# Convolution steps placed by a table of points, and the border terms at a later point, in a kernel of self-attention and local attention

## The chip, the cores and the metric

The kernel runs on one core of a Trainium2 chip. The metric is the device time of one execution in microseconds (us), the median of three; lower is better. In the trace the engines are PE (TensorE, matmuls), PEld (its weight loads), DVE (VectorE), ACT (ScalarE), POOL (GpSimd) and SP (SyncE, which issues transfers).

## What is computed

Two layers on an image batch of 4 x 64 x 64 points with 256 channels, all in float32. The reference, cut to what matters:

```python
# layer 0: attention of every point of an image to every other
q, k, v = x @ Wq + bq, x @ Wk + bk, x @ Wv + bv        # 256 -> 32, 32, 256
attn = softmax(einsum('bnd,bmd->bnm', q, k))           # 4096 x 4096 per image
x = gamma * (attn @ v) + x

# layer 1
perceived = depthwise_conv3x3(x, w_perc) + b_perc      # 3 outputs per channel: 768
hid = gelu(w_up1 . perceived + b_up1)                  # 768 -> 512
h = x + (w_up2 . hid + b_up2)                          # 512 -> 256
q, k, v = split(w_qkv . h + b_qkv)
scores = [(q * k shifted by (dy, dx)).sum(-1) / 16 for the 9 neighbours, zeros outside]
out = h + sum(softmax(scores)[i] * v shifted by i)
```

## The kernel before

**Slots and points.** The image rows are worked in blocks of 8 rows (512 points), 8 blocks to an image, so 32 slots in all. Slot `s` runs layer 0's attention for block `s`, and with it layer 1's stages for earlier blocks: the convolution for block `s - 2`, the pointwise layers, guides and scores for block `k = s - 3`, the local attention's output for block `a = s - 5`. [...]

A slot has 16 points. At each point the program issues, in this order: the energies of keys two points ahead (`energy`, every other point, line 294); the exponential of them on ACT (`weight`, L302); the jobs of layer 1 listed for this point; `product`, the attention product of this point (4 matmuls, each of which stands as two records, L313, tile `acc`); the sum of the weights on DVE (`add_up`, L327, tile `den`); and then a number of convolution steps on DVE. At the end of the slot the sums are turned and inverted and the finished block is written back to the image buffer `xp`.

**The convolution.** `perceive` hands out single DVE instructions. A tap is a multiply-add of a shifted window (L468), a tile of 6 outputs by 8 taps: 48 in a slot. The ninth tap of an output is its first, done on ACT with the bias (`begin`, L464), and is issued when the step after it is asked for. The outputs come in three groups of two, each group in one `perc` buffer; after the 16 taps of a group come 4 additions or subtractions (L474, "mixes"), which prepare the operands of a matrix product by Strassen's scheme with 7 products (Winograd's form). So a group is 20 steps, and a slot 60. There are four `perc` buffers: group 1 of a block takes the one that held group 0 of the block before, which the first pointwise layer (`hidden_part`, points 0 to 3) reads.

**The jobs by point.** For block `k` the two pointwise layers and the guides (the product of query and key weights, applied to `h`) are done in parts named for their products:

| point | jobs | |
|---|---|---|
| 0 to 3 | `hidden_part`: products a, bc, then de, gf, for d = 0 and d = 1 | DVE gathers them (L580), ACT applies GELU (L596) |
| 4, 5 | `local_product` for block a: the output's two halves, `lo` | DVE scales (L1026), POOL adds up for a check and adds `h` (L186, L1036) |
| 5 | `update_mix` | DVE (L660, L661) |
| 6 to 8 | `update_part`: dx_ab, dx_cd and dx_eg, dx_f | DVE gathers into `h` (L537); with ab also L678 and L679, which replace two blocks of `hid` by mixes of them |
| 8 | end of part f: bias and residual (L689), `guide_mix` (L798), `border_terms` (L855, L856) | DVE |
| 9, 10 | `guide_part`: g_ab, g_cd, then g_eg, g_f | DVE gathers into `lq` (L537, L539) |
| 11, 12 | `scores`, halves 0 and 1 (tile `s`, L924) | ACT exponential, POOL mask and sums |
| 13 | `local_values` (L883) | |
| 14 | `border`: a matmul over the tile `edge`, which `border_terms` writes | ACT, POOL |

`border_terms` works out the score of the points outside the image: two DVE instructions for each of two sides, and for each of two halves of a row more in the first and the last block of an image (4 instructions, or 8).

The second pointwise layer's product cd reads the blocks of `hid` that L678 writes in part ab; g_cd reads the tiles `gmix` of `guide_mix`; the scores read `lq`.

In the last block of each of the first three images the next image's projections (query, key and value, L226 and L260) are done in the same slot, every other point: slots 7, 15 and 23.

The lines that set the convolution's pace, before:

```python
n_mixed = NPC * (TAPS - 1) + MULT * len(MIXED)      # 60
to = min(n_steps, -(-(point + 1) * n_steps // (points - 2)))
if point < 3:
    to = min(to, n_mixed // MULT)
while stepped < to:
    next(conv, None)
    stepped += 1
```

## Time and profile before

The kernel takes 3490.17 us (3489.78 to 3491.19). The profiled execution has a span of 3487.6 us.

| what | value |
|---|---|
| PE busy | 3454.0 us, 99% of the span |
| PEld busy | 1995.1 us, 57% |
| DVE busy | 2796.8 us, 80% |
| ACT busy | 1063.4 us, 30% |
| POOL busy | 694.3 us, 20% |
| granted PE clock | 0.999 |
| L313 attention product | 4096 records, 1838.6 us |
| L468 convolution taps | 1554 instructions, 1166.7 us, mean 0.811 us |
| L474 convolution mixes | 360 instructions, 174.3 us, mean 0.498 us |
| L327 sum of the weights | 480 instructions, 604.6 us, mean 1.259 us |
| transfers | mean 19 GB/s |

Matmuls are pipelined and their ends are modelled, so the busy share of PE covers short waits; they are read from the distance between starts in the timeline. In the timeline a line gives the start in us, the length of the merged stretch, the engine, the line of the program, the operation, the output and inputs, the shape and the count, and in brackets the idle time before it with what ended it.

### The profile page before, as it was taken

To read this page: it belongs to the slowest core of one execution; us is meant where nothing else is said; L and a number is where in the kernel's file an instruction comes from. 1 tells how busy PE (TensorE), PEld (TensorE's weight loads), DVE (VectorE), ACT (ScalarE), POOL (GpSimd) and SP (SyncE) were. 2 spreads that over 40 slices of the span, in tenths; PEclk is the share of its full clock that TensorE was granted. 3 is DMA by queue.
4 is the path that set the end of the run, shared out by engine and by line. 5 is a ranking of instruction groups with operands and counts; after the bars stand their busy time and mean duration, and the time that the engine had idled before them with its cause. 6 is when DMAs were issued, how large, how long until landed. Compare 5 with 4: busy or idle time off the path is not lost. (4 is left out here: it accounts for less than half of the span.)

```text
span 3487.6 us, 34030 instructions
## 1 busy us (share of the span) xinstructions
PE 3454.0 (99%) x12726; PEld 1995.1 (57%) x12726; DVE 2796.8 (80%) x4249; ACT 1063.4 (30%) x1328; POOL 694.3 (20%) x829
## 2 busy tenths in 40 slices
PE   9999999999999999999999999999999999999998
PEld 5445555555555555566555555556655555555655
DVE  2388888768888988876888889887688888888886
ACT  3233333323332233332333322333233333223331
POOL 2010112111221221121112212212121121221133
PEclk9999999999999999999999999999999999999999
DMA  4000000120000000011000000001100000000000
GB/s 106 7 4 10 7 9 16 32 47 20 9 16 7 16 16 16 22 25 46 16 9 16 10 13 16 16 22 31 39 16 16 16 10 7 16 16 17 7 7 25
DMA packets 93276, 67.06 MB, mean 19 GB/s; under 512 B 65872, under 2 KB 71248, under 8 KB 92976
## 3 DMA queue, kind: packets, MB, share of 16 engines
q1 hardware_dynamic: 92432, 64.42, 6.8%
q8 instruction: 102, 1.67, 0.2%
q14 instruction: 70, 0.57, 0.1%
q10 hardware_dynamic: 672, 0.39, 0.0%
HBM read 43.62 MB, written 18.81 MB: 18 GB/s over the span
## 5 line engine op out<-in xcount | busy, mean ns | idle before, releaser
L313 PE MATMUL acc<-p,v 128*128 128x512 f32 x4096 | 1838.6, 594 | 0.2 <-DVE o L378 0.2
L313 PEld LDWEIGHTS acc<-p,v 128*128 128x128 f32 x4096 | 768.2, 190 | 795.8 <-issue 779.6
L468 DVE SCALAR_TENSOR_TENSOR perc<-xp,wperc,perc 128x512 f32<-128x512 f32 (+2 forms) x1554 | 1166.7, 811 | 7.0 <-ACT perc L464 7.0
L302 ACT ACTIVATE p<-e 128x1024 f32<-128x1024 f32 x512 | 523.9, 1023 | 1695.0 <-PE e L294 776.9
L327 DVE TENSOR_TENSOR den<-den,p 128x1024 f32<-128x1024 f32 x480 | 604.6, 1259 | 85.4 <-ACT p L302 83.6
L186 POOL TENSOR_TENSOR watched<-watched,lo 128x256 f32<-128x256 f32 x124 | 136.8, 1103 | 1015.8 <-DVE lo L1026 1010.7
L948 POOL TENSOR_TENSOR lp<-lp,near 128x396 f32<-128x396 f32 x60 | 77.5, 1291 | 1137.9 <-ACT lp L944 1132.9
L294 PE MATMUL e<-qa,ka 32*128 32x512 f32 x2048 | 291.9, 640 | 0.0
L474 DVE TENSOR_TENSOR perc<-perc 128x256 f32<-128x256 f32 x360 | 174.3, 498 | 7.2
L294 PEld LDWEIGHTS e<-qa,ka 32*128 32x128 f32 x2048 | 80.0, 182 | 166.2 <-issue 164.2
L573 PE MATMUL hid_de<-perc,wmix 128*128 128x256 f32 x720 | 165.2, 379 | 0.0
L573 PEld LDWEIGHTS hid_de<-perc,wmix 128*128 128x128 f32 x720 | 136.8, 190 | 43.7 <-issue 21.5
L580 DVE TENSOR_TENSOR hid<-hid_bc,hid 128x512 f32<-128x512 f32 x60 | 41.5, 692 | 147.4 <-PE hid_bc L573 147.3
L596 ACT ACTIVATE hid<-hid,bup 128x512 f32<-128x512 f32 x120 | 80.1, 715 | 214.3 <-DVE hid L580 214.3
L464 ACT ACTIVATE perc<-xp,bperc,wperc 128x512 f32<-128x512 f32 x192 | 145.4, 807 | 0.0
L969 POOL TENSOR_TENSOR lsum<-lsum,lp 128x99 f32<-128x99 f32 x168 | 132.0, 792 | 11.0
L1014 PEld LDWEIGHTS lo<-lp,lv 128*128 128x128 f32 x732 | 102.9, 191 | 35.1 <-issue 27.0
L883 PE MATMUL lv<-wlv,h 128*128 128x256 f32 x520 | 122.4, 379 | 0.0
L186 POOL TENSOR_TENSOR watched<-watched,o 128x256 f32<-128x256 f32 x128 | 109.6, 856 | 43.2 <-DVE o L378 35.7
L302 ACT ACT_TABLE_LOAD x60 | 77.0, 1283 | 134.1 <-PE e L294 134.1
L260 PE MATMUL v<-wv,xc 128*128 128x256 f32 x512 | 116.3, 380 | 0.1
L883 PEld LDWEIGHTS lv<-wlv,h 128*128 128x128 f32 x520 | 98.7, 190 | 27.5 <-issue 15.5
(191 smaller groups left out, 3398.8 us busy)
## 6 DMA issues: line engine op xcount, KB each, us to landing
xp<-in_x SPq DMA_DIRECT2D x30, 528.0 KB, 4.1
xc<-in_x SPq DMA_DIRECT2D x56, 256.0 KB, 3.7
out<-lo SPq DMA_DIRECT2D x56, 256.0 KB, 2.1
qa<-packed SPq DMA_DIRECT2D x124, 64.0 KB, 2.0
out<-res SPq DMA_DIRECT2D x8, 256.0 KB, 2.0
ka<-st SPq DMA_DIRECT2D x124, 16.0 KB, 1.8
packed<-st SPq DMA_DIRECT2D x31, 64.0 KB, 1.9
wup<-in_w_up SPq DMA_DIRECT2D x1, 1536.0 KB, 6.8
```

Of the source, the lines that this page charges most:

```text
L186: nc.gpsimd.tensor_tensor(at, at, values[:, i : min(n, i + C)], ALU.add)
L260: nc.tensor.matmul(ps[:, i * C : (i + 1) * C], lhsT=xc[:, kin, bass.ts(2 * pair + i, P)], rhs=wv[:, kin, :], start=(kin == 0), stop=(kin = ...
L294: nc.tensor.matmul(e[:, j, :], lhsT=key[rows, :], rhs=queries[s][rows, :], start=True, stop=True,)
L302: nc.scalar.activation(p, energies[s, G][:, 2 * half : 2 * half + 2, :], AF.Exp)
L313: nc.tensor.matmul(accs[s][c], lhsT=v[:, 2 * half + i, bass.ts(c, P)], rhs=p[:, i, :], start=(first and i == 0), stop=(G == NG - 1 and hal ...
L327: nc.vector.tensor_tensor(den, den, p, ALU.add)
L464: nc.scalar.activation(acc, win, AF.Identity, bias=bperc[:, half, j : j + 1], scale=wt)
L468: nc.vector.scalar_tensor_tensor(acc, win, wt, acc, ALU.mult, ALU.add)
L474: nc.vector.tensor_tensor(t[:, to, :], t[:, a, :], t[:, b, :], op)
L573: nc.tensor.matmul(ps[:, n * C : (n + 1) * C], lhsT=w(j), rhs=mixes[s, j][:, kind, :], start=(j == 0), stop=(j == MULT - 1),)
L883: nc.tensor.matmul(ps[:, half * C : (half + 1) * C], lhsT=keys_of(s, t, half, kin), rhs=wlv[:, kin, :], start=(kin == 0), stop=(kin == CH ...
L969: nc.gpsimd.tensor_tensor(to, to, near_ws[block, half][:, t_, of, :], ALU.add)
```

## The change

Two edits of order; no operation is added or dropped.

The pace of the convolution follows a table of steps per point instead of an even spread over 14 points, in all slots but the last. The table has few steps at points 6 to 9, where the second pointwise layer and the guides are done, and more at the points before. The spread before comes to 5, 4, 4, 5, 4, 4, 4, 5, 4, 4, 5, 4, 4 and 4 steps at points 0 to 13. It is meant to let DVE serve the products of points 6 to 10 sooner.

`border_terms` is no longer called at the end of `update_part`'s part f (point 8) but as a job of its own at point 13, ahead of `local_values`. The call in `update`, which serves the last blocks, stays.

```diff
@@ update_part
                 guide_mix(s)
-                border_terms(s)
@@ jobs
-                job(scores, k, 1) + job(local_sum, k - 1), job(local_values, k, 0), job(border, k), [],
+                job(scores, k, 1) + job(local_sum, k - 1),
+                job(border_terms, k) + job(local_values, k, 0), job(border, k), [],
@@ the slot's loop
             n_steps, stepped = n_mixed, 0
+            share = [7, 7, 6, 6, 6, 5, 2, 1, 1, 2, 3, 5, 5, 4, 0, 0]
...
-                to = min(n_steps, -(-(point + 1) * n_steps // (points - 2)))
+                if slot < NSLOT - 1:
+                    to = sum(share[: point + 1])
+                else:
+                    to = min(n_steps, -(-(point + 1) * n_steps // (points - 2)))
                 if point < 3:
                     to = min(to, n_mixed // MULT)
```

## The prediction

> **What bounds the kernel now.** I read the page's busy shares first, then the list of waits, then the timeline of one ordinary slot (slot 8, 786.7 to 889.8 us) engine by engine, and beside it a slot with a bordering block (slot 10).

> ```profile
> PE 3454.0 (99%) x12726; PEld 1995.1 (57%) x12726; DVE 2796.8 (80%) x4249; ACT 1063.4 (30%) x1328; POOL 694.3 (20%) x829
> ```

> TensorE is the bound: a slot takes what its matmuls take, plus the few places where they wait. Here is TensorE in slot 8 (start, length, operation), from point 3 to point 9:

> ```profile
> 819.51 3.60 PE L313 MATMUL acc<-p,v 128*128 128x512 f32 x8
> 835.37 1.99 PE L525 MATMUL dx_ab<-hid,wup 128*128 128x256 f32 x8
> 837.20 3.60 PE L313 MATMUL acc<-p,v 128*128 128x512 f32 x8
> 840.64 1.03 PE L525 MATMUL dx_cd<-hid,wmix 128*128 128x256 f32 x4
> 849.65 3.60 PE L313 MATMUL acc<-p,v 128*128 128x512 f32 x8
> 853.09 1.17 PE L525 MATMUL g_ab<-h,wg 128*128 128x256 f32 x4
> 854.84 1.10 PE L525 MATMUL g_cd<-gmix,gmix 128*128 128x256 f32 x4 [0.58 <-DVE gmix L798]
> ```

> The reader is to see two things. An acc group of eight is followed 3.44 us later by the next group: no wait before dx_cd. But g_ab to g_cd takes 1.75 us, where four such matmuls take 0.86 (dx_cd, 840.64 to 841.50): 0.89 us is waited for gmix. The same in slot 10 before the scores:

> ```profile
> 1069.79 1.88 PE L313 MATMUL acc<-p,v 128*128 128x512 f32 x4
> 1072.36 1.66 PE L924 MATMUL s<-lq,h 128*128 128x198 f32 x8 [0.70 <-DVE lq L539]
> ```

> Why gmix is late is on VectorE's timeline of slot 8:

> ```profile
> 819.71 0.69 DVE L580 TENSOR_TENSOR hid<-hid_gf,hid 128x512 f32<-128x512 f32 x1 [1.44 <-PE hid_gf L573]
> 820.32 1.22 DVE L327 TENSOR_TENSOR den<-den,p 128x1024 f32<-128x1024 f32 x1
> 821.45 2.07 DVE L468 SCALAR_TENSOR_TENSOR perc<-xp,wperc,perc 128x512 f32<-128x512 f32 x3
> 823.56 0.88 DVE L474 TENSOR_TENSOR perc<-perc 128x256 f32<-128x256 f32 x2
> 826.02 0.69 DVE L1026 TENSOR_TENSOR lo<-lo,lrden 128x512 f32<-128x512 f32 x1 [1.58 <-PE lo L1014]
> 829.50 2.42 DVE L468 SCALAR_TENSOR_TENSOR perc<-xp,wperc,perc 128x512 f32<-128x512 f32 x2
> 833.15 1.10 DVE L661 TENSOR_TENSOR hid<-hid 128x512 f32<-128x512 f32 x1
> 834.17 1.74 DVE L327 TENSOR_TENSOR den<-den,p 128x1024 f32<-128x1024 f32 x1
> 835.84 3.75 DVE L468 SCALAR_TENSOR_TENSOR perc<-xp,wperc,perc 128x512 f32<-128x512 f32 x4
> 839.51 0.68 DVE L678 TENSOR_TENSOR hid<-hmix,hid 128x512 f32<-128x512 f32 x1
> 848.19 3.40 DVE L468 SCALAR_TENSOR_TENSOR perc<-xp,wperc,perc 128x512 f32<-128x512 f32 x5
> 851.50 0.42 DVE L537 TENSOR_TENSOR h<-dx_f,h 128x256 f32<-128x256 f32 x1
> ```

> dx_f's matmuls end at 849.65, but its gather (L537) starts at 851.50, behind five convolution steps. These twelve lines carry the forecast as well: after its last idle 1.58 us before lo, VectorE works without a pause to L678, and L678 ends at 840.19. L678 writes the block that dx_cd's first matmul reads at 840.64. So dx_cd has about 0.45 us to spare, hardly more than the 0.15 us between gmix's end (854.69) and g_cd's start.

> [...] 99% busy holds the 0.89 us wait. [...] while GpSimd sums lo, one step starts at 829.50 and the next 1.68 us later, where steps elsewhere follow each other every 0.66 us.

> **The change, part by part.** Steps per point go from 5 4 4 5 4 4 | 4 5 4 4 | 5 4 4 4 to 7 7 6 6 6 5 | 2 1 1 2 | 3 5 5 4. The sum stays 60: 48 taps at 0.66 us and 12 mixes at 0.43. Nothing is removed, so only order can pay. The last slot keeps the old rule.

> *Few steps at points 6 to 9.* VectorE then reaches dx_f's gather before the matmuls end. From that gather to the third gmix it needs 3.19 us (851.50 to 854.69), say 3.4 from dx_f's end, while acc and g_ab give TensorE 3.44 + 0.86 = 4.30 us. The wait before g_cd goes. Counting every start-to-start distance above what the form needs when nothing waits, g costs 0.96 us and s 0.24 us of an ordinary slot more than in the three slots with projections, 7, 15 and 23. There are 23 full ordinary slots: 23 x 0.96 = 22.1.

> *Border's terms to point 13.* 4 instructions (8 in a bordering block) of some 0.2 us leave point 8, where they stand before the den sum and the guides' gathers. At point 13 VectorE has finished the guides, and border (matmul at point 14) is their only reader. With fewer steps at 9 and 10 the scores' wait goes too: 0.24 in 16 slots, 1.02 in six with a bordering block, 0.59 in slot 12, 0.88 in slot 3: 3.8 + 6.1 + 0.6 + 0.9 = 11.4. Gain so far 33.5 us.

> *More steps at points 0 to 2.* Hidden by VectorE's pauses: at point 0 two more taps are 1.3 us, the de gather comes at 802.2 instead of 800.8, and the hidden product that takes its bank starts at 806.9. At point 1 three more taps end at 809.8; the bc gather waits for TensorE until 811.17 anyway. At point 2, taps and four mixes end near 815.9, before de at 817.12. So point 3 starts as before. Cost nothing.

> *More steps at points 3 to 5.* Here there is no room. Before: 13 steps, 9 taps and 4 mixes. After: 17, of which 16 taps and one mix, since the four mixes of group 0 are done at point 2 and group 1 begins at point 3. Also, group 1's first taps are ScalarE's (L464), and at point 3 they now stand behind the two GELUs: these start at 820.44 and 821.07, so the first taps end near 822.5 and 823.2. They can't be earlier, as the perc buffer is free only after hid_gf. VectorE, ready at 821.45, waits 1.1 us. From 820.32:
> - point 3: den 1.13; wait 1.13; six taps 4.0 (the second waits a little): lo's scaling at 826.6, not 826.02.
> - point 4: scaling 0.61, den 1.13, six taps 3.97, and 1.94 lost to GpSimd (as in slot 8: L474 0.52 and 0.41, L468 1.01): the second scaling at 834.2, not 831.84.
> - point 5: scaling 0.60, hmix and L661 1.41, den 1.13, four taps 2.65, one mix 0.42, 1.94 lost to GpSimd: L678 at 842.3, not 839.51.
> L678 ends at 843.0, and with the 0.15 us of the g_cd release dx_cd starts at 843.15, not 840.64: a new wait of 2.5 us. Queued behind dx_cd on TensorE are eg, the next acc groups and everything else[...]. It isn't earned back: the slot behind it is matmuls back to back. In the projection slots TensorE has 3.6 to 5.5 us more at points 3 and 5, and VectorE idled 5.03 us before lo (slot 15), so no wait. Slots 3 and 4 have no lo and no GpSimd work there: I reckon 0.7 and 0.5. Bounds: were GpSimd's 3.9 us lost in pauses, no wait at all; with another 0.7 us for tap order and releases, 3.2 a slot. I take 2.5: 23 x 2.52 + 1.2 = 59.

> Sum: 3490.2 - 33.5 + 59 = 3516 us. An ordinary slot goes from 103.1 to 104.4 us.

> **Rivals.** (A) The early points keep up, the waits at g_cd and s vanish: 3490.2 - 33.5 = 3457. For it: VectorE is busy 89 of 103 us in a slot, so slack exists. Against: of that slack none lies between lo and L678 beyond 1.58 us. (B) The new wait is about 1.4 us, equal to the 33.5 us gained: 3490. It takes VectorE 1.1 us earlier at L678, for instance no wait for ScalarE's first taps; against it, their place behind the GELUs. (C) A larger loss: L678 later still, or a second wait (eg for hmix, exp for a p buffer) beside it: at 3.3 us a slot, 3490.2 - 33.5 + 77 = 3534. Against: dens run two or more points ahead of the buffers that exp takes.

> **Numbers.** Forecast 0.72, A 0.11, B 0.06, C 0.11. The forecast's own spread, 2.0 to 3.1 us per slot, is 3504 to 3529; with part of C up to 3534 and some room towards B, 3500 to 3534 holds 8 in 10. Slower takes the forecast and C: 0.83; within 0.2% is B with its edges: 0.06; faster 0.11.

> **What would show it.** Right: the timeline has dx_cd waiting some 2.5 us for L678 in the 23 ordinary slots, none before g_cd and at most a trace before s, the first L464 of group 1 directly after the GELUs with a VectorE pause near 1.1 us at point 3, slots of 104.4 us, and 137.0 with projections. Wrong: L678 before 840 in slot 8's time (then A), or a wait elsewhere, such as exp for p or a bank at points 0 to 2.

## The result and the profile after

The changed kernel takes 3546.11 us (3545.12 to 3548.19), the kernel before 3490.68 us in the same comparison: a ratio of 1.016, 95% interval 1.0142 to 1.0177. It is slower, as forecast, but by 55.4 us, where 26 us were forecast, and above the stated range of 3500 to 3534 us.

```profile
PE 3475.9 (98%) x12726; PEld 2022.4 (57%) x12726; DVE 2811.6 (79%) x4249; ACT 1063.4 (30%) x1328; POOL 653.9 (18%) x829
```

The shares on the page hardly move: TensorE goes from 99% to 98%, while the span grows by 57.2 us. The same stretch of slot 8 shows why. The slot now starts at 791.44 us. First VectorE from point 3 on, in the timeline:

```profile
825.09 1.22 DVE L327 TENSOR_TENSOR den<-den,p 128x1024 f32<-128x1024 f32 x1
827.28 4.11 DVE L468 SCALAR_TENSOR_TENSOR perc<-xp,wperc,perc 128x512 f32<-128x512 f32 x6 [0.98 <-ACT perc L464]
831.30 0.68 DVE L1025 TENSOR_TENSOR lo<-lo,lrden 128x512 f32<-128x512 f32 x1
833.04 6.01 DVE L468 SCALAR_TENSOR_TENSOR perc<-xp,wperc,perc 128x512 f32<-128x512 f32 x6
838.97 0.68 DVE L1025 TENSOR_TENSOR lo<-lo,lrden 128x512 f32<-128x512 f32 x1
842.97 3.73 DVE L468 SCALAR_TENSOR_TENSOR perc<-xp,wperc,perc 128x512 f32<-128x512 f32 x4
847.08 0.68 DVE L678 TENSOR_TENSOR hid<-hmix,hid 128x512 f32<-128x512 f32 x1
```

L678 starts 55.64 us after the start of the slot; in the kernel before it was 52.83 (839.51 - 786.68). It is 2.81 us later, behind the taps of points 3 to 5: in this stretch VectorE's instructions start in the order in which the program issues them (den 825.09, taps 827.28, lo 831.30 and so on to L678 847.08). Then TensorE in the same slot:

```profile
841.97 3.60 PE L313 MATMUL acc<-p,v 128*128 128x512 f32 x8
847.82 1.80 PE L525 MATMUL dx_cd<-hid,wmix 128*128 128x256 f32 x4 [2.26 <-DVE hid L678]
849.41 1.91 PE L525 MATMUL dx_cd<-hid,wup 128*128 128x256 f32 x4
851.12 1.25 PE L525 MATMUL dx_eg<-hmix,wmix 128*128 128x256 f32 x4
```

Two things are to be seen. dx_cd starts 5.85 us after the acc group began, instead of 3.44: it waits 2.42 us. (The bracket says 2.26, as it counts from the modelled end of the last matmul.) And the matmuls behind the wait are slow: the second group of four dx_cd takes 1.71 us to the next start (849.41 to 851.12), where the same four took 0.86 before. Slot 10, with the same wait, doesn't have this:

```profile
1060.04 1.13 PE L525 MATMUL dx_cd<-hid,wmix 128*128 128x256 f32 x4 [2.26 <-DVE hid L678]
1061.01 1.03 PE L525 MATMUL dx_cd<-hid,wup 128*128 128x256 f32 x4
```

The list of stretches of 3.41 us, cut so that the changes of the clock fall on the cuts, names it. Its columns are the stretch, its length, TensorE's busy time and instructions, the granted share of TensorE's clock, and two columns on transfers:

```profile
841.32:844.73 3.41, 3.41 (x11) 1.00 0.00 0
844.73:848.14 3.41, 1.15 (x3) 1.00 0.55 154
848.14:851.56 3.42, 3.42 (x10) 0.50 0.00 0
851.56:854.97 3.41, 3.41 (x13) 1.00 0.00 0
```

The stretch that holds the whole wait has TensorE busy for 1.15 us of 3.41. In the next 3.41 us the clock is halved, which costs 1.69 us (eight matmuls at 0.43 instead of 0.22 us). Comparing the starts of all 23 full ordinary slots: every one waits 2.42 to 2.44 us before dx_cd, 18 are halved once and take 106.1 us, and 5 (slots 5, 10, 16, 21 and 26) take 104.4. The waits before g_cd and before the scores are gone from the list of waits; it has instead

```profile
PE dx_cd L525 <- DVE hid L678: 52.9, 25, 2.3
```

### The profile page after: what moved, and what is told of

It is laid out like the page before. It is cut to its first block, busy times and chain, and to the rows that moved or that the text cites. A ratio compares the mean times of both kernels' runs of the same rounds, so it can differ in the third digit from the quotient of the medians.

```text
span 3544.8 us, 34087 instructions
## 1 busy us (share of the span) xinstructions
PE 3475.9 (98%) x12726; PEld 2022.4 (57%) x12726; DVE 2811.6 (79%) x4249; ACT 1063.4 (30%) x1328; POOL 653.9 (18%) x829
## 4 chain that ended last, share of the span: by engine, by line
PE 82%; DVE 15%; ACT 2%; issue 1%; POOL 0%; DMA 0%; SPq 0%; ACTq 0%; POOLq 0%; DVEq 0%
PE acc L313 40%; DVE perc L468 9%; PE e L294 6%; PE hid_gf L573 4%; PE hid_de L573 4%; PE hid_bc L573 4%; PE lv L882 3%; PE v L260 3%; PE hid_a L573 3%; PE s L923 2%; PE dx_cd L525 2%; DVE den L327 2%; PE dx_eg L525 2%; PE hid L605 1%; ACT hid L596 1%
## 5 line engine op out<-in xcount | busy, mean ns | idle before, releaser
L313 PE MATMUL acc<-p,v 128*128 128x512 f32 x4096 | 1838.6, 594 | 0.3 <-DVE o L378 0.3
L313 PEld LDWEIGHTS acc<-p,v 128*128 128x128 f32 x4096 | 768.2, 190 | 795.8 <-issue 779.8
L468 DVE SCALAR_TENSOR_TENSOR perc<-xp,wperc,perc 128x512 f32<-128x512 f32 (+2 forms) x1554 | 1174.6, 818 | 32.4 <-ACT perc L464 32.4
L327 DVE TENSOR_TENSOR den<-den,p 128x1024 f32<-128x1024 f32 x480 | 600.9, 1252 | 85.0 <-ACT p L302 83.2
L186 POOL TENSOR_TENSOR watched<-watched,lo 128x256 f32<-128x256 f32 x124 | 143.9, 1161 | 1063.2 <-DVE lo L1025 1058.1
L573 PE MATMUL hid_de<-perc,wmix 128*128 128x256 f32 x720 | 165.2, 379 | 0.0
L573 PEld LDWEIGHTS hid_de<-perc,wmix 128*128 128x128 f32 x720 | 136.8, 190 | 43.7 <-issue 21.5
L474 DVE TENSOR_TENSOR perc<-perc 128x256 f32<-128x256 f32 x360 | 146.4, 427 | 6.2
L464 ACT ACTIVATE perc<-xp,bperc,wperc 128x512 f32<-128x512 f32 x192 | 145.0, 803 | 0.0
L1013 PEld LDWEIGHTS lo<-lp,lv 128*128 128x128 f32 x732 | 102.9, 191 | 35.1 <-issue 32.5
L260 PEld LDWEIGHTS v<-wv,xc 128*128 128x128 f32 x512 | 96.9, 190 | 28.3 <-issue 14.6
L923 PEld LDWEIGHTS s<-lq,h 128*128 128x128 f32 x520 | 87.1, 188 | 37.2 <-issue 27.4
L1013 PE MATMUL lo<-lp,lv 128*128 128x99 f32 (+1 forms) x732 | 107.4, 295 | 0.0
```

The costliest lines, as they stand in the source:

```text
L186: nc.gpsimd.tensor_tensor(at, at, values[:, i : min(n, i + C)], ALU.add)
L260: nc.tensor.matmul(ps[:, i * C : (i + 1) * C], lhsT=xc[:, kin, bass.ts(2 * pair + i, P)], rhs=wv[:, kin, :], start=(kin == 0), stop=(kin = ...
L313: nc.tensor.matmul(accs[s][c], lhsT=v[:, 2 * half + i, bass.ts(c, P)], rhs=p[:, i, :], start=(first and i == 0), stop=(G == NG - 1 and hal ...
L327: nc.vector.tensor_tensor(den, den, p, ALU.add)
L468: nc.vector.scalar_tensor_tensor(acc, win, wt, acc, ALU.mult, ALU.add)
L474: nc.vector.tensor_tensor(t[:, to, :], t[:, a, :], t[:, b, :], op)
```

## The experiments

Times are medians, with the ratio to the kernel before on the same chip and its interval. Slot lengths are distances between the starts of the matmuls that close a slot (tile `dps`) in the timeline.

**Keeping TensorE busy during the wait.** Two matmuls of 512 columns go ahead of dx_cd into the bank that it overwrites, in the ordinary slots only:

```diff
+            for _ in range(fill):      # 2 for part cd, 0 otherwise
+                nc.tensor.matmul(ps, lhsT=ones, rhs=wup2[:, :2, :].rearrange("p k c -> p (k c)"),
+                                 start=True, stop=True)
```

> The changed kernel with two extra 512-column matmuls per ordinary slot (1.72 us) on TensorE just ahead of dx_cd, in the time in which it waits for L678 (2.42 us in the trace of the changed kernel). They write the bank that dx_cd then overwrites, so the result is untouched; VectorE's order is the same. Theory 1 (the wait itself brings the TensorE clock down afterwards): at most 0.7 us of TensorE idleness is left, no half-clock stage in the slots, dx_cd starts no earlier and no later than before, ordinary slots 104.4 us, total 3515 to 3518. Theory 2 (the half-clock stages have another cause, such as the load or a drift of this chip, and only coincide with the wait): they stay, total 3546 or more.

3516.19 us, 1.0075 (1.0058 to 1.0092). TensorE in slot 8, from its timeline (here L524 are the extra matmuls, L685 is the line of L678), and the mean clock of the run:

```profile
844.02 1.88 PE L524 MATMUL dx_cd<-wup,ones 128*128 128x512 f32 x4
846.44 1.13 PE L530 MATMUL dx_cd<-hid,wmix 128*128 128x256 f32 x4 [0.55 <-DVE hid L685]
847.41 1.03 PE L530 MATMUL dx_cd<-hid,wup 128*128 128x256 f32 x4
```

```profile
core 0: 3513.7 us, clock 0.999
```

The real dx_cd starts 56.38 us after the start of its slot (790.06), exactly as in the changed kernel (847.82 - 791.44). VectorE's order and the dependency are the same; only TensorE's idle time is filled, up to the 0.55 us in the bracket. No slot is halved, the ordinary slots take 104.4 us, and 30 us are gone. It isn't the chip: the version with the table alone (below), run on the same chip in the same set of runs, keeps 18 halved slots. The half-clock stages come from the idleness, and they are 30 of the 55 us.

**A longer and a shorter wait.** One mix more at point 5, or one fewer:

```diff
-            share = [7, 7, 6, 6, 6, 5, 2, 1, 1, 2, 3, 5, 5, 4, 0, 0]
+            share = [7, 7, 6, 6, 6, 6, 1, 1, 1, 2, 3, 5, 5, 4, 0, 0]   # longer
+            share = [7, 7, 6, 6, 6, 4, 3, 1, 1, 2, 3, 5, 5, 4, 0, 0]   # shorter
```

> The changed kernel with one mix more at point 5 and one fewer at point 6 (table ... 6 6 | 1 1 1 2 ...): L678 comes 0.46 us later, the wait before dx_cd is 2.88 us. Theory 1: the clock is halved for 3.41 us when a window of 3.41 us on a fixed grid holds more than some 2.15 to 2.3 us of the wait (the trace of the changed kernel: 2.15 us without, 2.30 us with). Stepping through the slots with these lengths (104.9 us, 106.6 after a halving) gives 11 to 13 halvings whatever the phase of the grid, instead of 18: 10.6 us more wait, some 10 us less half clock, total 3545 to 3549. Theory 2 (each wait of this length brings a halving, or the longer the wait the more of them): 23 halvings, total 3565.

> The changed kernel with one mix fewer at point 5 and one more at point 6 (... 6 4 | 3 1 1 2 ...): the wait before dx_cd is 2.0 us. Theory 1 (no window can then hold 2.15 us of it): no halving in the slots, ordinary slots 104.0 us, total 3505. Theory 2 (halvings in proportion to the wait): some 15 halvings, total 3530.

The shorter wait: 3504.96 us, 1.004 (1.0026 to 1.0055). The wait is 1.97 us, no slot is halved, an ordinary slot takes 104.0 us. Clear for theory 1.

The longer wait: 3554.64 us, 1.0183 (1.0166 to 1.02), between the two expectations. The wait is 2.88 us in all 23 slots, and 15 slots are halved, fewer than the 18 of the shorter wait of 2.42 us. So theory 2 falls; but theory 1's count of 11 to 13 is missed too. Going through the slots with the fixed grid: a stretch with 2.26 us of the wait (slot 21) is followed by a halving, one with 2.16 us (slot 11) is not. (These are the wait's own microseconds, up to the start of dx_cd; by the busy times of the list TensorE is idle 0.16 us less, as the ends of its matmuls are modelled.) Which slots are hit hangs on where the grid falls, and the count took a fixed price and one halving a slot; neither is so. In slots 21 and 29 the half clock lasts for two stretches:

```profile
2256.28:2259.69 3.41, 2.79 (x7) 2.25 (x8) 3.06 (x5) 0.00 (x0) 0.00 (x0) 0.50 0.00 0
2259.69:2263.10 3.41, 3.41 (x10) 2.70 (x9) 0.85 (x2) 0.00 (x0) 0.00 (x0) 0.50 0.00 0
```

(busy times here of PE, PEld, DVE, ACT, POOL, then the clock). There the first half-clock stretch still held 0.62 us of the wait; where it held 0.56 us or less, one stretch was all. What ends the half clock wasn't tried.

**Fewer steps at points 3 to 5.** The front of the table and the border terms stay:

```diff
-            share = [7, 7, 6, 6, 6, 5, 2, 1, 1, 2, 3, 5, 5, 4, 0, 0]
+            share = [7, 7, 6, 4, 4, 3, 2, 4, 1, 4, 5, 5, 4, 4, 0, 0]
```

> The changed kernel with the table 7 7 6 | 4 4 3 | 2 4 1 4 | 5 5 4 4: the first three points and the place of the border terms as in the change, fewer steps at points 3 to 5, so that L678 comes near 839.4 in the time of slot 8 of the kernel before (limit about 839.85), and 2 and 4 steps at points 6 and 7, which still end before dx_f. Theory 1 (the loss is made at points 3 to 5 alone): no wait before dx_cd, none before g_cd and s, ordinary slots near 101.9 us, total 3457, below both kernels. Theory 2 (the front-loaded points 0 to 2, or the border terms, carry part of the loss): total between 3480 and 3530, with a wait elsewhere.

3457.15 us, 0.9904 (0.9887 to 0.9921): faster than both kernels. VectorE and TensorE in slot 8 (start 783.72) in their timelines:

```profile
836.41 0.68 DVE L678 TENSOR_TENSOR hid<-hmix,hid 128x512 f32<-128x512 f32 x1
```

```profile
834.25 3.60 PE L313 MATMUL acc<-p,v 128*128 128x512 f32 x8
837.68 1.03 PE L525 MATMUL dx_cd<-hid,wmix 128*128 128x256 f32 x4
...
850.13 1.03 PE L525 MATMUL g_ab<-h,wg 128*128 128x256 f32 x4
850.99 1.03 PE L525 MATMUL g_cd<-gmix,gmix 128*128 128x256 f32 x4
```

dx_cd follows the acc group after 3.43 us, g_cd follows g_ab after 0.86: neither wait is left, and the slot takes 101.9 us, 1.2 less than before. L678 comes 52.69 us after the slot's start. The idea of the change holds; its table was too full at points 3 to 5: with the first three points as they were and the steps taken from there placed at points 7, 9 and 10, no wait is left.

**Each edit alone.** The border terms moved and the old spread kept; then the table kept and the border terms at point 8:

```diff
+                if False:                                  # first: always the even spread
-                if slot < NSLOT - 1:
@@ second
                 guide_mix(s)
+                border_terms(s)
...
-                job(border_terms, k) + job(local_values, k, 0), job(border, k), [],
+                job(local_values, k, 0), job(border, k), [],
```

> The kernel before with the border terms alone moved to point 13 (even spread of the steps). Theory 1 (they delay the guides' gathers by 0.9 or 1.7 us and stand behind the third gmix): the wait before s goes (0.24 us in 16 slots, 1.02 in six, 0.59 and 0.88 in two), the one before g_cd stays 0.9 us: total 3479. Theory 2 (the move brings a wait of its own at border or the local values): 3490 or more.

> The changed kernel with the border terms back at point 8. Theory 1 (the loss is the table's alone, and with few steps at points 8 to 10 the scores have room for the border terms too): within 3 us of the changed kernel's 3546. Theory 2 (the move has a part in the loss): below 3540.

The border terms alone: 3478.32 us, 0.9966 (0.9952 to 0.998), 12 us faster. Every ordinary slot takes 102.9 us (slot 6 103.0), with or without a bordering block, and the wait before g_cd is what it was in the kernel before, whose list of waits also has 13.4 us in 23 waits:

```profile
PE g_cd L525 <- DVE gmix L797: 13.4, 23, 0.7
```

The table alone: 3546.47 us, 1.0163 (1.0146 to 1.018), the changed kernel's time, again with 18 halved slots. The loss is the table's; with few steps at points 8 to 10 the border terms find room at either place.

**Two terms of the delay.** The first taps of group 1, issued on ScalarE ahead of point 3's GELUs; and GpSimd's check sums of lo left out, so that only its addition of `h` stands there:

```diff
@@ perceive
+            starts[s] = begin
@@ hidden_part, ahead of the GELUs
+                if d == 1 and s + LAG_HID < NSLOT - 1:
+                    starts[s + 1](1)               # the first tap, on ScalarE
+                    starts[s + 1](1 + MULT)
@@ local_product
-            if s < NSLOT - 1:
-                watch(o)
```

> The changed kernel with the first taps of group 1 on ScalarE ahead of point 3's two GELUs instead of behind them. Theory 1 (VectorE's pause of 1.0 us at point 3 is a term of the loss, but 0.5 us of it is given back, as VectorE must wait for lo's matmuls then): L678 0.5 us earlier, the wait 1.9 us, below what halves the clock: total 3501 to 3505. Theory 2 (the pause is covered by something else): total 3540 or more.

> The changed kernel without GpSimd's two sums of each half of lo (the check of lo's range is left out; the addition of h stays). Theory 1 (each of these sums holds VectorE up by 0.41 to 0.53 us between lo and L678, 1.9 us in all): wait before dx_cd 0.6 us, no halving, total 3472 to 3476. Theory 2 (the slow steps there are slow for another reason than GpSimd): total 3540 or more.

The first taps early: 3503.77 us, 1.0039 (1.0024 to 1.0053). The wait before dx_cd is 1.91 us (2.27 in one slot), no slot is halved. VectorE's pause at point 3 has gone, but half of it is given back ahead of lo:

```profile
822.17 4.06 DVE L471 SCALAR_TENSOR_TENSOR perc<-xp,wperc,perc 128x512 f32<-128x512 f32 x6
826.74 0.69 DVE L1031 TENSOR_TENSOR lo<-lo,lrden 128x512 f32<-128x512 f32 x1 [0.51 <-PE lo L1019]
```

L678 half a microsecond earlier in each slot is 42 us on the kernel: 23 x 0.51 = 12 of it are shorter waits, and nearly all the rest is the clock (30).

Without the check sums: 3471.21 us, 0.9945 (0.9928 to 0.9961), just below the 3472 to 3476 expected. The six taps at point 4, 6.01 us in the changed kernel, take

```profile
827.30 5.07 DVE L468 SCALAR_TENSOR_TENSOR perc<-xp,wperc,perc 128x512 f32<-128x512 f32 x6
```

and the wait before dx_cd is 0.48 us, so the sums held VectorE up by 1.94 us between lo and L678 (2.42 - 0.48).

## Why the prediction was right in kind and wrong in size

- *The waits removed.* Right. 33.5 us were worked out for g_cd and the scores; the version with no new wait is 32.9 us faster in its own comparison (3490.05 - 3457.15). The part given to the border terms and the scores, 11.4 us, measured 11.7 with the border terms moved alone (3490.05 - 3478.32).
- *More steps at points 0 to 2 cost nothing.* Right: they stay in the fastest version.
- *More steps at points 3 to 5.* Right in place and length: L678 2.8 us later as worked out, the wait 2.42 us against 2.52, VectorE's pause for ScalarE's first taps 1.0 us against 1.1. Of the 3.9 us put down to GpSimd, the half that belongs to its sums is shown by leaving them out (1.94 us); its addition of `h` stayed in every run. The line read as "while GpSimd sums lo" (829.50) is such an addition: GpSimd's own timeline has the sums from 826.86 and the addition (L1036) from 829.37.
- *The projection slots, and slots 3 and 4.* Right: 137.0 us and no wait; 0.76 and 0.45 us in slots 3 and 4, where 0.7 and 0.5 were reckoned.
- *The failed step: "a new wait of 2.5 us", priced at its own length.* The term 23 x 2.52 + 1.2 = 59 took it that the matmuls behind the wait run as fast as ever, and with it the sentence "An ordinary slot goes from 103.1 to 104.4 us". That holds in 5 slots only. In 18 the wait also brought the clock to half for 3.41 us: 18 x 1.69 = 30.4 us that the sum doesn't have. With TensorE kept busy the kernel takes 3516.19 us, the 3516 forecast; with the 30.4 us it comes to 3546.6, against 3546.11 measured. That 104.4 and 3516 are met so closely has some luck in it: the wait is 0.1 us shorter than worked out, but the first matmul behind it takes 0.32 us to the next start instead of 0.22, which the sum doesn't have either. The rivals didn't have the clock: (C) looked for a larger loss in a longer or a second wait.

What could have been seen: in the trace of the changed kernel each of the 18 half-clock stages in the slots is 3.41 us long, and all of them start on one grid of 3.413 us (605.80, 848.14 and 953.96 us, for instance, are 71.00 and 31.00 steps apart). The stretch ahead of such a stage wasn't idle throughout: in the one above TensorE was busy for 1.15 us of 3.41. Before the change no ordinary slot had a wait over 0.70 us by the brackets, and the page, with its clock of 0.999, couldn't show it. But the trace of the kernel before does have such a stage, in the last block: the stretch from 3415.83 to 3419.24 us, in which TensorE works on short matmuls (`ld`) and is busy for 1.90 us, is followed by 3.41 us at half the clock:

```profile
3415.83:3419.24 3.41, 1.90 (x13) 1.00 0.00 0
3419.24:3422.65 3.41, 3.41 (x5) 0.50 0.00 0
```

The second price could have been found there.

## What to carry to other kernels

## What the runs showed that was not expected

- The halving follows a fixed grid of 3.41 us: a wait of 2.42 us escapes it when the grid cuts it so that neither part is above about 2.2 us (2.15 and 2.16 us without a halving; 2.20, in slot 14 of the table alone, 2.26 and 2.30 with one). A longer wait, 2.88 us, was halved in fewer slots (15 against 18). The border is that of this place in the slot, not a general one: in the last block of the kernel before, by the busy times, 1.51 us of idleness among short matmuls was enough, where 2.00 us in slot 11 of the longer wait was not. What exactly sets the halving off stays open.
- The grid and the slots lock. A halved slot of 106.11 us is 31.09 steps of the grid, so the next slot's wait falls only 0.3 us later in its step: in slots 12 to 14 it begins 0.18, 0.48 and 0.79 us into it. That is why 18 of 23 were hit, in the changed kernel and with the table alone, where at random some 10 would be (an estimate: with the border at 2.2 us, 1.43 us of the 3.41 us of positions are hit).
- A change in VectorE's timing of 0.4 to 0.5 us a slot moved the kernel by 41 to 42 us (3546 to 3505 and 3504), over three times the sum of the times saved.
